# A selective scan and a convolution with attention, float32 on one core: the first layer's gates are stored before silu, and a new order is planned batch by batch

## The chip, the core and the metric

The kernel runs on one core of a Trainium2 chip. Engines are named as in the profile: PE (TensorE, matrix products and transposes), DVE (VectorE), ACT (ScalarE), POOL (GpSimd) and SP (SyncE, which here only issues DMAs). All data are float32. The metric is the device time of one execution in microseconds (us); lower is better.

## The reference

The input x is (4, 512, 32, 32): four batches, 512 channels, 1024 tokens. Two layers, each added to its input after a group normalisation `_gn`:

```
x = x + L0(_gn(x))      # selective scan
x = x + L1(_gn(x))      # convolutions and attention
# L0, per batch, 1024 tokens, 1024 inner channels, 16 states
xm, z = layernorm(x) @ W_in, split in two
xs    = silu(conv1d(xm, 4 taps) + conv_b)
dt    = softplus(xs @ W_x[:, :32] @ W_dt + b_dt);  Bm, Cm = the other 32 columns
h[t]  = exp(dt[t] * A) * h[t-1] + (dt[t] * xs[t]) * Bm[t]      # 16 states a channel
y     = sum over states of h * Cm + xs * D
out   = (y * silu(z)) @ W_out
```

L1 is a 3x3 convolution, an attention over the 1024 tokens by two 1x1 convolutions, and another 3x3 convolution; its 3x3 convolutions are done with transformed filters.

## The kernel before, in words

**Tiling of the first layer.** Channels lie on the 128 partitions, so the 1024 inner channels are 8 chunks d, taken in pairs e; the 1024 tokens are two halves h of 512. A *group* is (batch b, pair e, half h) and does 16 *units*, one for each state s; 4 x 4 x 2 x 16 = 512 units.

**A unit** (`unit`, L844 to L951) has one of two forms, by the table `ACT_B` in `shares` (L302). *On ACT*: ACT scales the transposed dt·x by the state's B, four instructions (L875); PE turns the result back into a `u` bank of PSUM, eight transposes (L901); ACT writes the decay exp(dt·A) (L862). *Off ACT*: POOL multiplies dt·x by a broadcast row of B that SP loads (`bbc`, L890), and ACT writes the decay into the `u` banks. Then DVE scans, two instructions (L915). The product with C is POOL's (L938, one instruction for both chunks) or, for as many of the off-ACT units as `DVE_C` says, DVE's (L931, two), which then also copies the carry (L920). PE adds each chunk's product, transposed, into the banks `y0` and `y1` (L948).

**The end of a group** (`gate`, L956 to L1003): SP loads the pair's gates for this half (`szl`, L965), ACT copies y0 and y1 into one tile `yt` (L971), PE turns each into an `mm` bank (L981), DVE adds xs·D (L988) and multiplies by the gates (L991), and SP stores the result (`gd`, L1000). In the last batch the product stays in `xs`.

**Gates** (`gates`, L727): for each chunk, PE projects both halves (`pz`), ACT copies them into `sz` (L735) and takes silu of the whole (L739), and SP stores it to DRAM (`szd`, L743). The gates of batch b + 1 are made during batch b.

**Other work in the layer**: `norms` (group and layer norm), `conv1` and `conv1_half` (projection, four taps, silu at L685 and L723), `params` (B, C and dt's inputs), `delta` (softplus at L813, dt·x, its transposes), `out_proj` and `last_proj` (W_out), `transform` (18 pieces of the second layer's filters, on POOL, L1208 to L1228, as filler) and `first_image`. Softplus, silu and exp need different tables on ACT; a load is recorded at the line that asks for it, and a return to exp at L210.

**What sets the order.** Nothing is issued where it is written: each `step` goes to a planner (`Plan`, L60 to L172) with its engine, an assumed duration, a priority (a lower number is more urgent; unit s of group n of batch b has 128 b + 16 n + s) and the buffers it takes. `issue` (L108) plays the engines forward with these durations, with `LAG` and `HOP` between engines, `LOAD` for a table and `kb / 300 + 2.0` for a DMA, and issues the steps in the order that results. `AHEAD` bounds how far a step may run before the most urgent open one. A step that needs another table is put back by 5.46 x 1.3 unless it is more urgent than the others by 2.66. On the chip each engine, SP too, then runs its own list in order and waits where data or buffers are late. `PRM` holds the offsets of the priorities, `slots` the buffers of each ring: `mm` 2 and `u` 4 (PSUM), `y0` and `y1` one each, `sz`, `szl`, `yt` 1, `h` and `dbx` 4, `cbc` 5, `bb` 3, `xt` 1.

**The start.** Before the plan, L214 to L345 issue loads: `gmat` and x on SP, `w_top`, `w_center` and their biases on POOL (L223 to L227), and on ACT the two bias rows `brow` (L233), each scaled by -12 on ACT (L236), then nine small ones (`small`, L313, and L331 and L338). ACT takes exp of `a_log` (L327) and DVE negates it (L328).

Of the kernel before, what the change touches and what calls it, by code (L numbers as in the profile page):

```python
# [30 lines left out]
PRM = dict(tf=-22.1, pg=0.35, kt=2.5, ke=2.06, ka=-1.93, fl=0, fi=-4.54, m0=42.67, n0=49.76, nl=1.48, q0=67.23, qg=4.59, c0=60.23, cg=6.17, p0=114.55, e0=1.02, eg=7.73, g0=80.83, gg=9.09, o0=14.49, og=6.33, dl=12.15, t0=8, tg=57.65)  # L31


ACT_B = ((12, 9, 10, 9, 9, 10, 9, 9), (11, 9, 12, 8, 9, 8, 8, 8), (9, 9, 12, 12, 11, 12, 12, 13))
DVE_C = ((4, 7, 5, 1, 2, 3, 5, 5), (4, 3, 3, 2, 1, 5, 2, 4), (4, 4, 4, 4, 3, 1, 4, 2))
# [24 lines left out]
class Plan:  # L60
# [4 lines left out]
    LAG = {"PE": 0.2, "DVE": 0.08, "ACT": 0.1, "POOL": 0.06, "SP": 0.0}  # L65
    HOP, LOAD, SLACK, AHEAD = 0.05, 1.3, 0.11, 15.09
# [41 lines left out]
    def issue(self):  # L108
        ready = {e: [s for s in self.steps if s.eng == e and not s.unmet] for e in self.ENGINES}
        clock = {e: 0.0 for e in self.ENGINES}  # L110
# [4 lines left out]
        while left:  # L115
# [4 lines left out]
            for e in self.ENGINES:  # L120
                urgent = min((s.prio for s in ready[e] if s.table in (None, table)), default=1e9)
                found = []
                for s in ready[e]:
# [9 lines left out]
                    wait = t + (5.46 * self.LOAD if late and s.prio > urgent - 2.66 else 0.0)  # L133
# [25 lines left out]
            for b in s.bufs:  # L159
                b.left -= 1  # L160
                if b.ring and not b.left:
                    free[b.ring].append(s.done + self.HOP)
                    if b.done:
                        b.done(b.tile)
            ready[s.eng].remove(s)
            for u in s.users:
                u.unmet -= 1
                other = u.eng != s.eng or s.kb
                u.ready = max(u.ready, s.done + self.HOP if other else clock[s.eng])
                if not u.unmet:  # L170
                    ready[u.eng].append(u)
# [4 lines left out]
def mamba_then_pab_kernel(  # L176
# [46 lines left out]
    nc.gpsimd.dma_start(wt_sb[:, :, 0, :], w_top.rearrange("(c p) n -> p c n", p=P))  # L223
    nc.gpsimd.dma_start(wt_sb[:, :, 1, :], w_center.rearrange("(c p) n -> p c n", p=P))
    pb_sb = cpool.tile([P, 1], F32, tag="pb", name="pb_sb")
    nc.gpsimd.dma_start(pb_sb[0:PAB], b_top)
    nc.gpsimd.dma_start(pb_sb[PAB:P], b_center)  # L227


    brow = []  # L230
    for name, src in (("b", b_bottom), ("o", b_out)):
        t = cpool.tile([1, C], F32, tag=f"brow_{name}", name=f"brow_{name}")
        nc.scalar.dma_start(  # L233
            t.rearrange("o (c p) -> o c p", p=P), src.rearrange("p (c o) -> o c p", o=1)
        )
        nc.scalar.activation(t, t, AF.Copy, scale=-12.0)  # L236
        brow.append(t)
# [46 lines left out]
    with ExitStack() as l0:  # L284
# [7 lines left out]
        first_x = xtp.tile([P, NCC, L], F32, tag="xt", name="xt_0", bufs=1)  # L292
        for c in range(NCC):
            nc.sync.dma_start(first_x[:, c, :], x[0, c * P : (c + 1) * P].rearrange("p h w -> p (h w)"))

# [6 lines left out]
        def shares(b, n):  # L302

            k = min(b, 1) + (b == B - 1)
            rest = NS - ACT_B[k][n]
            off = [int((i + 0.5) * (NS - 1) / rest) for i in range(rest)]
            c = DVE_C[k][n]
# [20 lines left out]
        nc.vector.tensor_scalar_mul(a_sb, a_sb, -1.0)  # L328
# [21 lines left out]
        def dram_set(name, shape, n=B):  # L350
# [8 lines left out]
            "xt": 1, "xs": 10, "win": 2, "yt": 1, "dt": 2, "dtx": 2, "dtxt": 2, "cbc": 5,  # L359
            "sc": 2, "h": 4, "sz": 1, "bb": 3, "dbx": 4, "szl": 1, "wpr": 2, "res": 2,  # L360
# [7 lines left out]
        MM, TR = 0.88, 0.114  # L368
        ROWS, EXP, SCAN = 0.8, 0.61, 1.18
# [27 lines left out]
        xts, ready, xs, xh, dts = {}, {}, {}, {}, {}  # L397
# [21 lines left out]
        def norms(b, prio, lag=0.0):  # L419

            t = xts[b] = buf("xt", [P, NCC, L], f"xt_{b}")
            if b == 0:
                t.make = lambda: first_x
            src = x[b].rearrange("(c p) h w -> p c (h w)", p=P)
            xin = [buf(None, None, "") for c in range(NCC)]
            step("SP", 0.0, lambda: t(), [], [], prio, holds=[t])
            for c in range(NCC):
                step(
                    "SP", 0.3,
                    lambda c=c: b and nc.sync.dma_start(t()[:, c, :], src[:, c, :]),  # L430
                    [], [xin[c]], prio, kb=512, holds=[t],
                )
# [6 lines left out]
            for c in range(NCC):  # L439
# [9 lines left out]
                step("DVE", 1.4, stats, [xin[c]], [stat], prio, holds=[t])  # L449
# [15 lines left out]
            step("DVE", 0.6, mid, [], [pm, stat], prio)  # L465
# [47 lines left out]
            step("PE", 0.6, shift_mean, [stat], [pv], prio)  # L513
# [61 lines left out]
            for h, (r, pvar) in enumerate(zip(rs, pvars)):  # L575
                at = prio if b else at_half[h]
                step(
                    "ACT", 0.58,
# [74 lines left out]
        def conv1(b, d, prio):  # L653
# [5 lines left out]
            for at, end in ((0, 341), (341, 682), (682, L)):  # L659
# [22 lines left out]
                step("DVE", 0.25 + n * 0.0042, taps, [p], xsh, prio, holds=[u])  # L682
            step(
                "ACT", 1.06,
                lambda: nc.scalar.activation(u(), u(), AF.Silu, bias=cb_sb[:, d : d + 1]),  # L685
                [], xsh, prio, "silu", holds=[u],
# [40 lines left out]
        def gates(b, d, prio):  # L727

            w = load_win(b, NDC + d, prio)
            sz = buf("sz", [P, L], f"sz_{b}_{d}")  # L730
            for h, hs in enumerate(halves):
                p = project(b, NDC + d, w, f"pz_{b}_{d}_{h}", hs, prio)
                step(
                    "ACT", 0.48,
                    lambda hs=hs, p=p: nc.scalar.copy(sz()[:, hs], p()),  # L735
                    [p], [sz], prio,
                )
            step(
                "ACT", 0.97, lambda: nc.scalar.activation(sz(), sz(), AF.Silu),  # L739
                [], [sz], prio, "silu",  # L740
            )
            step(
                "SP", 0.3, lambda: nc.sync.dma_start(szd[b][d // 2][:, d % 2, :], sz()),  # L743
                [sz], [szds[b][d]], prio, kb=512,
            )

        def params(b, prio, hh=tuple(range(NH))):
# [4 lines left out]
            for n, h in enumerate(hh):  # L752
                hs = halves[h]
                pp = buf("mm" if b or h else "y0", [P, T], f"pp_{b}_{h}")
                for d in range(NDC):
# [7 lines left out]
                        prio + PRM["pg"] * (d + NDC * n) if b else prio - 0.05 * (NDC - d),  # L763
# [979 lines left out]
```

## Time and profile before

| | us |
|---|---|
| Median of three runs | 2928.78 (2926.93 to 2932.84) |
| The profiled execution | 2926.95 |
| Its span, first to last instruction | 2925.1 |
| End of the first layer's last group (second `yt` copy) | 1886.9 |
| From there to the end | 1038.2 |
| PE busy in the span | 2724.9 |
| DVE busy | 2292.1 |
| POOL busy | 2045.6 |
| ACT busy | 1831.1 |
| Loads of ACT tables, 153 of 1.283 | 196.3 |

The span is cut in 40 equal slices of 73 us, and a digit is the busy share of a slice in tenths, 9 for 90% or more. A line of a group of instructions reads: line, engine, operation, output<-inputs with shapes and count | busy us, mean ns of one | idle us of the engine just before them, and who ended it.

### The profile page before, as it was taken

How to read it: one execution, taken by the hardware profiler on the slowest of the kernel's cores; microseconds unless marked ns; L12 is line 12 of the kernel's file. 1: busy time of each engine (PE TensorE's matmuls, PEld its weight loads, DVE VectorE, ACT ScalarE, POOL GpSimd, SP SyncE). 2: the span in 40 equal slices, each digit the busy share in tenths (PEclk: the TensorE clock that was granted, in tenths of full speed). 3: DMA queues.
4: the chain of work that ended last, by engine and by line, in shares of the span. 5: the costliest groups of instructions: out<-in, count | busy, mean ns of one | idle time of the engine just before them, and what ended most of it. 6: DMA issues, size and time to landing. Idle time of an engine off the chain costs nothing.

```text
span 2925.1 us, 36166 instructions
## 1 busy us (share of the span) xinstructions
PE 2724.9 (93%) x11712; PEld 1615.4 (55%) x11712; DVE 2292.1 (78%) x2719; ACT 1831.1 (63%) x3248; POOL 2045.6 (70%) x1247
## 2 busy tenths in 40 slices
PE   5988899999899999899999989799999999999998
PEld 2456566666666666666656666544444444444444
DVE  4679899988999989999979999867776655346254
ACT  4689899998799999889998999630200003030000
POOL 6899898899998999998999999733141341214222
PEclk9999899999999999999999999999999999999999
DMA  6856555467545577655567654757789886536487
GB/s 168 235 155 199 165 158 166 152 213 242 195 140 165 172 213 246 200 150 152 175 204 216 219 172 147 160 217 263 256 277 290 307 329 242 200 124 236 162 319 259
DMA packets 405348, 603.94 MB, mean 206 GB/s; under 512 B 46088, under 2 KB 245000, under 8 KB 380584
## 3 DMA queue, kind: packets, MB, share of 16 engines
q1 hardware_dynamic: 396352, 587.11, 62.5%
q10 hardware_dynamic: 8648, 14.26, 1.4%
q8 instruction: 94, 1.54, 0.2%
q14 instruction: 94, 0.77, 0.1%
q0 software_dynamic: 160, 0.26, 0.0%
HBM read 504.53 MB, written 96.99 MB: 206 GB/s over the span
## 4 chain that ended last, share of the span: by engine, by line
PE 34%; DVE 7%; POOL 6%; ACT 5%; issue 3%; DMA 2%; SPq 0%; DVEq 0%; POOLq 0%; ACTq 0%
PE m_o L1533 11%; PE m_b L1533 8%; PE pat L1585 6%; POOL da L938 2%; PE y L948 2%; PE po L412 2%; DVE da L915 2%; PE u L901 1%; ACT sc L875 1%; PE psc L1385 1%; ACT da L862 1%; POOL dbx L890 1%; DMA uw_o<-u_o 1%; POOL dbx L938 1%; DMA u_o<-wr 1%
## 5 line engine op out<-in xcount | busy, mean ns | idle before, releaser
L938 POOL TENSOR_TENSOR da<-da,cbc 128x1024 f32<-128x1024 f32 x313 | 739.9, 2369 | 46.1 <-DVE da L915 32.8
L875 ACT ACTIVATE sc<-dtxt,bt_sb 128x256 f32<-128x256 f32 x1252 | 550.5, 498 | 22.6 <-PE u L901 21.6
L890 POOL TENSOR_TENSOR dbx<-dtx,bbc 128x1024 f32<-128x1024 f32 x199 | 469.9, 2371 | 26.5 <-PE y L948 12.9
L862 ACT ACTIVATE da<-dt,a_sb 128x512 f32<-128x512 f32 x626 | 431.2, 713 | 25.4 <-PE y L948 24.4
L915 DVE TENSOR_TENSOR_SCAN da<-da,u 128x512 f32<-128x512 f32 x328 | 383.8, 1203 | 26.2 <-PE u L901 16.9
L901 PE MATMUL u<-ident,sc 128*128 128x128 f32 x2504 | 363.0, 277 | 34.1 <-DVE da L915 13.8
L948 PE MATMUL y<-ident,da 128*128 128x128 f32 x2504 | 348.8, 279 | 48.9 <-POOL da L938 45.8
L901 PEld LDWEIGHTS u<-ident,sc 128*128 128x128 f32 x2504 | 293.5, 142 | 168.3 <-issue 64.3
L915 DVE TENSOR_TENSOR_SCAN da<-da,carry_sb,u 128x512 f32<-128x512 f32 x298 | 365.2, 1259 | 19.8 <-PE u L901 15.6
L948 PEld LDWEIGHTS y<-ident,da 128*128 128x128 f32 x2504 | 287.7, 143 | 132.3 <-POOL da L938 101.6
L1533 PE MATMUL m_o<-uw_o,v_o 128*128 128x512 f32 x768 | 336.4, 597 | 8.3 <-DMA uw_o<-u_o 8.2
L1533 PE MATMUL m_b<-uw_b,v_b 128*128 128x512 f32 x768 | 333.7, 593 | 4.8 <-ACT e_b L1541 2.2
L862 ACT ACTIVATE u<-dt,a_sb 128x512 f32<-128x512 f32 x398 | 264.9, 681 | 13.9 <-DVE da L915 8.9
L412 PE MATMUL pxm<-xt,winc 128*128 128x345 f32 (+3 forms) x704 | 240.9, 485 | 11.2 <-DMA winc<-in_w_in_dram 4.0
L1533 PEld LDWEIGHTS m_o<-uw_o,v_o 128*128 128x128 f32 x768 | 145.3, 191 | 190.9 <-issue 179.8
L1533 PEld LDWEIGHTS m_b<-uw_b,v_b 128*128 128x128 f32 x768 | 144.9, 190 | 189.9 <-issue 178.9
L412 PE MATMUL pz<-xt,winc 128*128 128x512 f32 x512 | 244.0, 596 | 6.0 <-DMA winc<-in_w_in_dram 2.0
L948 PE MATMUL y<-ident,dbx 128*128 128x128 f32 x1592 | 221.0, 276 | 8.7 <-POOL dbx L938 7.3
L938 POOL TENSOR_TENSOR dbx<-dbx,cbc 128x1024 f32<-128x1024 f32 x93 | 220.6, 2372 | 10.7 <-DMA bbc<-bcd 5.4
L1585 PE MATMUL pat<-y_b,st 128*128 128x512 f32 x512 | 223.3, 597 | 1.6 <-DVE rz L1594 1.6
L948 PEld LDWEIGHTS y<-ident,dbx 128*128 128x128 f32 x1592 | 183.3, 142 | 49.5 <-POOL dbx L938 19.6
L1541 ACT ACTIVATE e_o<-m_o 128x512 f32<-128x512 f32 x24 | 14.3, 597 | 276.8 <-PE m_o L1533 276.8
(229 smaller groups left out, 4259.2 us busy)
## 6 DMA issues: line engine op xcount, KB each, us to landing
cbc<-bcd SPq DMA_DIRECT2D x512, 256.0 KB, 3.7
uw_b<-u_b SPq DMA_DIRECT2D x96, 1024.0 KB, 4.8
uw_o<-u_o SPq DMA_DIRECT2D x96, 1024.0 KB, 4.8
bbc<-bcd SPq DMA_DIRECT2D x199, 256.0 KB, 4.0
u_b<-work SPq DMA_DIRECT2D x192, 128.0 KB, 2.8
winc<-in_w_in_dram SPq DMA_DIRECT2D x72, 256.0 KB, 3.9
szd<-sz SPq DMA_DIRECT2D x32, 512.0 KB, 3.6
szl<-szd SPq DMA_DIRECT2D x32, 512.0 KB, 5.1
```

Source lines behind the costliest of these rows:

```text
L412: lambda k=k, lhs=lhs, rhs=rhs: nc.tensor.matmul(p()[:, at : at + cols], lhs(), rhs(), start=(k == 0), stop=(k == n - 1)),
L862: nc.scalar.activation(t, dt()[:, j], AF.Exp, scale=a_sb[:, at : at + 1])
L875: nc.scalar.activation(sc()[:, k], dtxt()[:, k], AF.Copy, scale=bt[:, at, s : s + 1])
L890: lambda: nc.gpsimd.tensor_mul(hc(), dtx(), b_bc().to_broadcast([P, 2, T])),
L901: nc.tensor.transpose(u()[:, k * P : (k + 1) * P], sc()[:, k, j, :], ident)
L915: nc.vector.tensor_tensor_scan(ht, *((hc()[:, j], u()) if on_act else (u(), hc()[:, j])), carry_sb[:, j, s : s + 1] if h else 0.0, ALU.mul ...
L938: nc.gpsimd.tensor_mul(hc(), hc(), c_bc().to_broadcast([P, 2, T]))
L948: nc.tensor.matmul(y[j]()[:, k, :], hc()[:, j, k * P : (k + 1) * P], ident, start=(s == 0 and k == 0), stop=(s == NS - 1 and k == NK - 1), ...
L1385: nc.tensor.matmul(pt, top[:, m * P : (m + 1) * P], center[:, h * T : (h + 1) * T], start=True, stop=True,)
L1533: nc.tensor.matmul(m[q], v[:, q, k, c, :], w[:, c, :], start=(c == 0), stop=(c == NCC - 1 and not extra),)
L1541: nc.scalar.activation(e, m[2], AF.Copy, scale=al / 2)
L1585: nc.tensor.matmul(pt, st[m][:, 2 * P * j + h : 2 * P * (j + 1) : 2], xb[m // 2][:, m % 2, :], start=(m == 0), stop=(m == NMC - 1),)
```

## The change

It does six things in the first layer.

1. **Gates.** `gates` copies each half from PSUM into a tile `z` of 512 columns and stores it raw. A new step, `gate_inputs`, loads a pair of chunks, both halves, into `sz` (2 x 1024 columns) and takes silu there in one instruction; both halves' groups use it. The buffers: `z` one, `sz` one, `szl` none.
2. **`yt`** is one tile for each chunk in place of one for both, and its ring still has one buffer, now of half the size.
3. **The convolution's silu** is a step of its own, for one or two chunks at a time (`xp`: two for batches 1 and 3, one for batch 2).
4. **Shares.** `ACT_B` and `DVE_C` have a row for each batch. On ACT: 77, 73, 73, 90 units before, 70, 74, 73, 90 after. C products on DVE: 32, 24, 24, 26 before, 33, 30, 32, 28 after.
5. **Order.** Offsets for each batch, a priority for each filter piece, new durations, lags and hops, engines that start at other times, and 1.06 in place of 5.46 for another table.
6. **Small loads.** The second layer's weights and biases are loaded by SP within the plan at priority 300, and the bias rows are scaled by ACT after the plan; x's first load is a step of the plan at priority -100; `a_sb` is negated on ACT.

The diff's core (the steps whose durations alone change are left out):

```diff
-PRM = dict(tf=-22.1, pg=0.35, kt=2.5, ke=2.06, ka=-1.93, fl=0, fi=-4.54, m0=42.67, n0=49.76, nl=1.48, q0=67.23, qg=4.59, c0=60.23, cg=6.17, p0=114.55, e0=1.02, eg=7.73, g0=80.83, gg=9.09, o0=14.49, og=6.33, dl=12.15, t0=8, tg=57.65)
-ACT_B = ((12, 9, 10, 9, 9, 10, 9, 9), (11, 9, 12, 8, 9, 8, 8, 8), (9, 9, 12, 12, 11, 12, 12, 13))
-DVE_C = ((4, 7, 5, 1, 2, 3, 5, 5), (4, 3, 3, 2, 1, 5, 2, 4), (4, 4, 4, 4, 3, 1, 4, 2))
+PRM = dict(
+    zl=(17.12, 2.32, 10.64, 9.46),
+    zs=(-6.6, 6.76, 2.95, 4.73),
+    xp=(2, 1, 2),
+    d1=4.6,
+    pg=(0.27, 0.49, 0.44, 0.21),
+    kt=(4.63, 8.03, 4.61, 4.92),
+    ke=(1.37, 5.31, 5.42, 3.82),
+    ka=(-2.99, -1.21, -2.32, -1.96),
+    dl=(11.98, 8.7, 12.71, 6.84),
...
+    g0=(-2.52, -46.63, -47.32, -52.32),
+    gg=(7.13, 9.33, 9, 9.19),
...
+    pc=(-90.27, -21.17, 5.21, -51.1, -41.83, -34.43, -45.01, 14.16, -32.58, 66.75, 105.34, 148.87, 209.89, 261.18, 327.32, 394.8, 432.73, 495.28),
...
+)
+ACT_B = (
+    (11, 9, 11, 9, 8, 7, 7, 8),
+    (11, 8, 13, 8, 8, 7, 10, 9),
+    (11, 8, 10, 10, 11, 7, 8, 8),
+    (9, 12, 10, 12, 11, 11, 11, 14),
+)
+DVE_C = (
+    (5, 4, 3, 4, 3, 2, 8, 4),
+    (4, 6, 3, 2, 2, 6, 2, 5),
+    (5, 4, 5, 2, 2, 6, 3, 5),
+    (7, 2, 3, 4, 3, 2, 5, 2),
+)
-    LAG = {"PE": 0.2, "DVE": 0.08, "ACT": 0.1, "POOL": 0.06, "SP": 0.0}
-    HOP, LOAD, SLACK, AHEAD = 0.05, 1.3, 0.11, 15.09
+    LAG = {"PE": 0.17, "DVE": 0.095, "ACT": 0.1, "POOL": 0.06, "SP": 0.0}
+    HOP = {"PE": 0.16, "DVE": 0.045, "ACT": 0.06, "POOL": 0.08, "SP": 0.05}
+    BEGIN = {"PE": 5.0, "DVE": 1.5, "ACT": 9.0, "POOL": 7.0, "SP": 1.5}
+    FREE, LOAD, SLACK, AHEAD = 0.06, 1.3, 0.11, 15.64
+    TURN, URGENT = 1.06, 2.68
-                    wait = t + (5.46 * self.LOAD if late and s.prio > urgent - 2.66 else 0.0)
+                    wait = t + (self.TURN * self.LOAD if late and s.prio > urgent - self.URGENT else 0.0)
+    def load_l1():
+        for k, w in enumerate((w_top, w_center)):
+            nc.sync.dma_start(wt_sb[:, :, k, :], w.rearrange("(c p) n -> p c n", p=P))
...
+        for t, src in zip(brow, (b_bottom, b_out)):
+            nc.sync.dma_start(
+                t.rearrange("o (c p) -> o c p", p=P), src.rearrange("p (c o) -> o c p", o=1)
+            )
-        nc.vector.tensor_scalar_mul(a_sb, a_sb, -1.0)
+        nc.scalar.activation(a_sb, a_sb, AF.Copy, scale=-1.0)
-            "xt": 1, "xs": 10, "win": 2, "yt": 1, "dt": 2, "dtx": 2, "dtxt": 2, "cbc": 5,
-            "sc": 2, "h": 4, "sz": 1, "bb": 3, "dbx": 4, "szl": 1, "wpr": 2, "res": 2,
+            "xt": 1, "xs": 10, "win": 2, "dt": 2, "dtx": 2, "dtxt": 2, "cbc": 5,
+            "sc": 2, "h": 4, "sz": 1, "z": 1, "yt": 1, "bb": 3, "dbx": 4, "wpr": 2, "res": 2,
         def gates(b, d, prio):
             w = load_win(b, NDC + d, prio)
-            sz = buf("sz", [P, L], f"sz_{b}_{d}")
             for h, hs in enumerate(halves):
                 p = project(b, NDC + d, w, f"pz_{b}_{d}_{h}", hs, prio)
...
+                z = buf("z", [P, T], f"z_{b}_{d}_{h}")
+                step("ACT", 0.468, lambda z=z, p=p: nc.scalar.copy(z(), p()), [p], [z], prio)
+                step(
+                    "SP", 0.3,
+                    lambda z=z, hs=hs: nc.sync.dma_start(szd[b][d // 2][:, d % 2, hs], z()),
+                    [z], [szds[b][d]], prio, kb=256,
+                )
+        def gate_inputs(b, e):
+            prio = (b * NDC + 2 * e) * NS + PRM["zl"][b]
+            sz = szs[b, e] = buf("sz", [P, 2, L], f"sz_{b}_{e}")
+            step(
+                "SP", 0.3, lambda: nc.sync.dma_start(sz(), szd[b][e]),
+                szds[b][2 * e : 2 * e + 2], [sz], prio, kb=1024,
+            )
+            step(
+                "ACT", 1.99, lambda: nc.scalar.activation(sz(), sz(), AF.Silu),
+                [], [sz], prio + PRM["zs"][b], "silu",
+            )
         def gate(b, e, h, y):
-            yt = buf("yt", [P, 2, NK, P], f"yt_{name}")
+            sz = szs[b, e]
+            yt = [buf("yt", [P, NK, P], f"yt_{name}_{j}") for j in range(2)]
             for j in range(2):
                 step(
-                    "ACT", 0.48, lambda j=j: nc.scalar.copy(yt()[:, j], y[j]()),
-                    [y[j]], [yt], prio - 0.5,
+                    "ACT", 0.468, lambda j=j: nc.scalar.copy(yt[j](), y[j]()),
+                    [y[j]], [yt[j]], prio - 0.5,
                 )
...
         norms(0, -20)
+        step("SP", 1.6, load_l1, [], [], 300, kb=64)
...
+                if not h:
+                    gate_inputs(b, e)
                 for s in range(NS):
                     unit(b, e, h, s, y)
...
             plan.issue()
+        for t in brow:
+            nc.scalar.activation(t, t, AF.Copy, scale=-12.0)
```

## The prediction, made before the changed kernel was run

> **What bounds the kernel now.** I read the busy tenths first: the first layer fills the first 26 slices, the second the other 14, where PE alone is full.
>
> ```profile
> span 2925.1 us, 36166 instructions
> ...
> PE   5988899999899999899999989799999999999998
> ...
> DVE  4679899988999989999979999867776655346254
> ACT  4689899998799999889998999630200003030000
> POOL 6899898899998999998999999733141341214222
> ```
>
> In the first layer PE, DVE, ACT and POOL are all at eight or nine tenths: no single bound, but four that take turns. So I cut it where a group of 16 units ends, at the second of its two `yt` copies in ACT's timeline: after the first group (198.7) and after batches 0, 1, 2 and 3 (600.6, 1052.0, 1506.9, 1886.9). Busy times by stage, columns us and (x instructions):
>
> ```profile
> core 0: us, PE busy (x) PEld busy (x) DVE busy (x) ACT busy (x) POOL busy (x), PEclk, DMA share, GB/s
> 198.70:600.60 401.90, 366.68 (x2011) 252.55 (x2010) 376.65 (x448) 389.19 (x669) 357.72 (x209) 0.97 0.55 168
> 600.60:1052.00 451.40, 423.44 (x2298) 288.13 (x2296) 411.56 (x474) 414.24 (x727) 423.70 (x255) 0.98 0.61 189
> 1052.00:1506.90 454.90, 426.72 (x2310) 292.17 (x2310) 408.17 (x468) 418.78 (x731) 429.11 (x262) 0.99 0.61 188
> 1506.90:1886.90 380.00, 343.49 (x2131) 252.49 (x2130) 364.88 (x394) 346.76 (x667) 371.74 (x229) 0.98 0.63 189
> ```
>
> Batch 0 is **ACT's** (12.7 idle of 401.9); batches 1 and 2 are PE's and POOL's together (26 to 28 idle), ACT and DVE 36 to 47; batch 3 is POOL's (8.3 idle), DVE next (15.1).
>
> Third, the groups of instructions, which give the prices (busy us, mean ns, idle before):
>
> ```profile
> L938 POOL TENSOR_TENSOR da<-da,cbc 128x1024 f32<-128x1024 f32 x313 | 739.9, 2369 | 46.1 <-DVE da L915 32.8 <-POOL carry_sb L937 0.2
> L875 ACT ACTIVATE sc<-dtxt,bt_sb 128x256 f32<-128x256 f32 x1252 | 550.5, 498 | 22.6 <-PE u L901 21.6
> L931 DVE TENSOR_TENSOR dbx<-u,cbc 128x512 f32<-128x512 f32 x212 | 138.6, 670 | 0.0
> L210 ACT ACT_TABLE_LOAD x67 | 86.0, 1283 | 1.8 <-PEq L1733 0.7
> L739 ACT ACT_TABLE_LOAD x29 | 37.2, 1283 | 0.5
> ```
>
> Mean times overlap with their neighbours, so I price by busy over count: a unit's B-scaling on ACT is four L875, 4 x 0.440 = 1.76; a POOL product 2.37; a unit's C-product on DVE two L931, 1.31; one of the 8 transposes that an ACT unit needs 363.0/2504 = 0.145 (L901); a table load 1.283. Last, the waits of the first 30 us:
>
> ```profile
> ACT brow_b L236 <- DMA brow_b<-in_b_bottom_dram: 12.0, 1, 12.0
> ...
> DVE a_sb L328 <- ACT a_sb L327: 4.6, 1, 4.6
> ```
>
> **What the Trainium skill says.** "ScalarE: Activation LUTs", What ACT_TABLE_LOAD costs: 1283 ns per load plus about 1380 ns of drain. The load agrees; the drain does not show (load at 24.99, next activation at 26.29), so I price 1.283. The same section gives an activation with immediate operands 186 + 0.833 N ns: 1039 at N = 1024, where the gates' silu shows 1059 (33.9/32). "GPSIMD Engine Reference", 4.1 Engine selection: two-input elementwise work is about twice as slow on GpSimd; here 2.37 for 1024 columns against 1.31, so a product moved to DVE takes less than it gives. "DMA: Bandwidth & Descriptors", Rules for kernel authors: a load whose last dimension isn't contiguous becomes one descriptor per element; the two 2 KB rows of `brow` show it, still awaited at 13.96 after an issue at 0.76, with the next load on ACT's queue held 8.45 in its issue.
>
> **The change, part by part**, against the profiled run (2926.95, span 2925.1; the median shown is 2928.78, so 1.8 is added at the end).
>
> *Start (to 198.7).* Now ACT waits for `brow` until 13.96, and the loads issued behind it on its queue, `a_log` among them, land late. Its exponential runs at 19.35, DVE's negation waits 4.6 for it, and the last statistics (data done at 15.07) stand behind that, at 19.84. With `brow` gone and the negation on ACT they follow at about 15.1: 4.7 gained. Then ACT stands 4.4 for the first filter piece, whose load SP held 8.4 for `lnw`; that load goes with the rest: ACT was ready for the logarithm at 22.06 and ran its table load at 24.99. 4.7 + 2.9 = 7.6 at most. x itself shares the transfers with the now earlier small loads: 0 at least. I take **-6**.
>
> *Batch 0 (198.7 to 600.6).* ACT: the shares of groups 1 to 7 fall from 65 to 59 units, 6 x 1.76 = 10.6. Silu: 12 singles here (6 of them for batch 1's gates) become three of batch 0's pairs; a pair costs 1.059 + 1024 x 0.833 ns = 1.91, so 12.7 - 5.7 = 7.0. Table loads: now 18 L210, 12 L739, 8 L685, 7 L813 = 45; after, 3 gate pairs, 4 convolution pairs, 7 softplus = 14, each with at most one return, 28: 17 x 1.283 = 21.8. ACT 389 - 39 = 350. POOL takes the 6 units: +6 x 2.36 = 14, 372. DVE keeps 28 C-products, 377. PE 6 x 8 x 0.145 = -7, 360. DVE becomes the bound, and ACT's saving beyond 12 is worth nothing. With 12.7 idle, as the bound has now, 389 (-12); with DVE's present 25, no gain: **-7**. If the table loads stay, ACT is at 372 and still not the bound.
>
> *Batch 1.* Shares 73 to 74, C-products on DVE 24 to 30. POOL -7 x 2.37 = -16.6 (407), DVE +7.9 (420), ACT about -4 (four loads fewer; the unit's 1.8; silu -0.8) (410), PE +1.2 (425). PE stays: only its waits for POOL can shrink: **-2**.
>
> *Batch 2.* C-products 24 to 32, and one filter piece (12.0: three L1208-like of 1.82 and nine of 0.73) goes to batch 3: POOL -31 (398), DVE +10.5 (419), ACT -10 loads and -0.8 = -14 (405), PE 427. **-5**.
>
> *Batch 3.* POOL +12.0 for the piece (priority 394.8, past 384), -2 x 2.37: +7.3 (379); DVE +2.6 and copies of carries +1 (368.5); ACT four pairs 7.6 for two silus 2.1 and about five loads 6.4: +12 (359, cover: 33 idle). POOL is the bound: +7, less what batch 2's freed POOL does ahead: **+4**.
>
> *Waits added.* The gate store is split: 32 issues more on SP, 16 gate loads fewer, 6 B-rows more (0.32 each, in SP's waiting time). `z` has one buffer: the second half's copy waits for the first half's store, and behind it on ACT stand exponentials and scalings, while `pz` holds one of two `mm` banks: 0 to 32 x 1 us; I take 0, since the priorities put other work between. The six small loads on SP in mid-layer can hold `cbc` loads up to 12 once; five `cbc` buffers cover five units of 3.5 us: 0, and 12 if that cover is used up. The two `brow` scalings (1.26) go into ACT's idle 3.1 ahead of L1433. `yt` has one half-buffer: see the slower rival; 0 in the sum. SP's x loads stay first.
>
> *Order.* The lags, hops and durations by which the planner orders everything change, and offsets become each batch's own. The trace of before cannot show it. The bounds' idle time is 12.7 + 28 + 26 + 8 = 75; batch 3 shows 2% is possible. Bounds -40 (batches 1 and 2 at batch 3's share) and +20 (a worse order by a quarter); I take **-16**.
>
> Sum: -6 - 7 - 2 - 5 + 4 - 16 = -32: 2926.95 - 32 + 1.8 = **2897**. The second layer (1038.2 to the end) is untouched.
>
> **The rivals.**
> *PE takes over.* For: PE is within 1 us of POOL in batch 1 and loses nothing there. Then batches 0 to 2 give nothing, batch 3 costs 7, the start gives 6: 2926.95 + 1 + 1.8, about 2930. Against: 45.8 of PE's waits are for POOL's L938.
> *The order pays fully.* Batches 1 and 2 idle like batch 3: -6 - 12 - 18 - 18 - 2 = -56, 2873. For: the filler pieces and gates have slack. Against: those batches carry projections through two `mm` banks, which batch 3 does not.
> *Slower: the serial drain of y.* ACT's second `yt` copy now waits until PE has turned the first. At 490.96 both copies run back to back (1.05), and the first four turns end at 493.92; with 0.58 for the copy y1 would come free at 494.5 instead of 492.0, 2.5 late. PE runs in order; its adds into y1, and POOL and DVE behind their tiles, wait. 31 boundaries x 2.5 = 78 at most, 2975; the gain of 32 is gone from 1.0 each on. I take half of it, 2897 + 39 = 2936. Against: PE can turn at once and other work fills in.
>
> **How the numbers follow.** Forecast 0.58 (own range 2880 to 2920), full order 0.20, PE takes over 0.10, drain 0.12. About 0.2% (6 us) is what can be told from no change. Faster 0.58 + 0.20 = 0.78, same 0.10, slower 0.12. The range 2866 to 2930 leaves out the drain and the far end of the full order.
>
> **What would show it.** Table loads about 100 to 130 in place of 153; ACT no longer the busiest of batch 0; the last statistics near 15; batch 3 longer by some us; the second `yt` copy no more than 1 us later than now. Wrong if PE's waits for ACT's `yt` exceed 30 us, if ACT waits for `z`'s store, or if the binding engine's idle time in batches 1 and 2 stays above 28.

## The result and the profile after

Over 20 executions of each, the changed kernel takes 2921.68 us (2913.54 to 2929.93) and the kernel before 2926.71: a ratio of 0.9984, interval 0.9975 to 0.9993. It is about 5 us faster; the forecast was 32. The profiled execution of after took 2919.48 (span 2917.7) against 2926.95, so its trace accounts for 7.4.

The page of after, busy tenths in 40 slices:

```profile
span 2917.7 us, 36108 instructions
...
PE   6888899999999999999999998799999999999998
...
DVE  4679999998999889999999899967777665346264
ACT  4779998898898898998999999630200003030000
POOL 6889999998988899988999999733141341214222
```

The picture is that of before: 26 slices in which four engines are nearly full. The first layer cut at the same places, the second `yt` copy of a group (L1012 now):

```profile
core 0: us, PE busy (x) PEld busy (x) DVE busy (x) ACT busy (x) POOL busy (x), PEclk, DMA share, GB/s
...
202.80:596.30 393.50, 357.28 (x1948) 248.59 (x1947) 378.58 (x455) 350.44 (x617) 369.19 (x212) 0.97 0.56 172
596.30:1052.40 456.10, 429.40 (x2324) 295.69 (x2323) 420.63 (x492) 412.30 (x725) 412.17 (x252) 0.97 0.59 187
1052.40:1492.90 440.50, 419.74 (x2304) 289.87 (x2303) 421.18 (x501) 402.77 (x712) 402.69 (x237) 0.99 0.63 194
1492.90:1881.90 389.00, 348.40 (x2116) 254.27 (x2114) 362.05 (x395) 360.59 (x672) 371.05 (x231) 0.98 0.62 183
1881.90:2917.70 1035.80, 1005.93 (x2428) 450.52 (x2428) 615.52 (x766) 136.47 (x241) 304.61 (x142) 0.99 0.71 248
```

Two columns are to be read against each other. The busy times came out nearly as worked out: batch 0 was to be PE 360, DVE 377, ACT 350, POOL 372, and is 357, 379, 350, 369; batches 1 to 3 are within 8 of the forecast on every engine. The lengths did not follow. What the busiest engine leaves idle is 393.5 - 378.6 = 14.9 (DVE), 26.7 (PE), 19.3 (DVE) and 17.9 (POOL): 79 in all, where before it was 12.7 + 28 + 26 + 8 = 75. The forecast took 16 out of that.

| stage | before | after | difference | forecast, without Order |
|---|---|---|---|---|
| to the first group's end | 198.7 | 202.8 | +4.1 | -6 |
| batch 0 | 401.9 | 393.5 | -8.4 | -7 |
| batch 1 | 451.4 | 456.1 | +4.7 | -2 |
| batch 2 | 454.9 | 440.5 | -14.4 | -5 |
| batch 3 | 380.0 | 389.0 | +9.0 | +4 |
| second layer | 1038.2 | 1035.8 | -2.4 | 0 |

So -7.4 = -32 + 16 (Order, which did not come) + 10 (the start) - 2 (second layer) + 1 (the batches: -9.1 for -10). Each length is read from one trace. Three more traces of kernels that do the same work in the same order in the first group (`loads_back`, `brow_late` and `brow_late_two`, below) end it at 198.9, 198.6 and 200.1 in place of 202.8, so a stage of a single trace is good to some 4 us, and the smaller differences of the table are not clear of chance.

The groups that the parts were priced by:

```profile
L983 POOL TENSOR_TENSOR da<-da,cbc 128x1024 f32<-128x1024 f32 x307 | 725.5, 2367 | 43.7 <-DVE da L960 24.2
L920 ACT ACTIVATE sc<-dtxt,bt_sb 128x256 f32<-128x256 f32 x1228 | 538.9, 498 | 50.5 <-PE u L946 49.5
L976 DVE TENSOR_TENSOR dbx<-u,cbc 128x512 f32<-128x512 f32 x246 | 161.2, 672 | 0.0
L252 ACT ACT_TABLE_LOAD x60 | 77.0, 1283 | 1.7 <-PEq L1783 0.7
L788 ACT ACTIVATE sz<-sz 128x2048 f32<-128x2048 f32 x16 | 30.6, 1911 | 0.2
```

Returns to exp fell from 67 to 60, all table loads from 153 to 125 (by batch 25, 34, 30 and 21, before 45, 40, 40 and 15); a pair's silu takes the 1.91 that was estimated. And ACT's scalings now wait 49.5 for PE's transposes (L946), where before they waited 21.6: ACT's idle time grew where its work shrank.

### The profile page after: what moved, and what is told of

Same layout as the page of the kernel before. It is cut to its first block, busy times and chain, and to the rows that moved or that the text cites. A ratio compares the mean times of both kernels' runs of the same rounds, so it can differ in the third digit from the quotient of the medians.

```text
span 2917.7 us, 36108 instructions
## 1 busy us (share of the span) xinstructions
PE 2726.0 (93%) x11664; PEld 1622.0 (56%) x11664; DVE 2319.7 (80%) x2776; ACT 1791.6 (61%) x3181; POOL 2018.2 (69%) x1220
## 4 chain that ended last, share of the span: by engine, by line
PE 48%; DVE 26%; ACT 9%; POOL 6%; issue 6%; DMA 5%; SPq 0%; DVEq 0%; ACTq 0%; POOLq 0%
PE m_o L1583 11%; PE m_b L1583 8%; DVE da L960 8%; PE pat L1635 6%; PE y L993 5%; DVE u L960 4%; PE u L946 4%; PE pz L447 3%; DVE dbx L960 3%; DVE xs L709 3%; PE po L447 3%; POOL da L983 2%; ACT sc L920 2%; ACT da L907 2%; DVE dbx L976 2%
## 5 line engine op out<-in xcount | busy, mean ns | idle before, releaser
L983 POOL TENSOR_TENSOR da<-da,cbc 128x1024 f32<-128x1024 f32 x307 | 725.5, 2367 | 43.7 <-DVE da L960 24.2
L920 ACT ACTIVATE sc<-dtxt,bt_sb 128x256 f32<-128x256 f32 x1228 | 538.9, 498 | 50.5 <-PE u L946 49.5
L935 POOL TENSOR_TENSOR dbx<-dtx,bbc 128x1024 f32<-128x1024 f32 x205 | 483.7, 2369 | 19.1 <-PE y L993 9.8
L907 ACT ACTIVATE da<-dt,a_sb 128x512 f32<-128x512 f32 x614 | 420.9, 713 | 23.0 <-PE y L993 21.6
L946 PE MATMUL u<-ident,sc 128*128 128x128 f32 x2456 | 368.1, 282 | 44.1 <-DVE da L960 25.2
L960 DVE TENSOR_TENSOR_SCAN da<-da,u 128x512 f32<-128x512 f32 x320 | 375.1, 1204 | 27.4 <-PE u L946 16.2
L946 PEld LDWEIGHTS u<-ident,sc 128*128 128x128 f32 x2456 | 291.2, 144 | 188.3 <-issue 64.6
L960 DVE TENSOR_TENSOR_SCAN da<-da,carry_sb,u 128x512 f32<-128x512 f32 x294 | 360.8, 1261 | 17.1 <-PE u L946 13.1
L993 PE MATMUL y<-ident,da 128*128 128x128 f32 x2456 | 341.1, 278 | 24.5 <-POOL da L983 22.2
L907 ACT ACTIVATE u<-dt,a_sb 128x512 f32<-128x512 f32 x410 | 272.2, 681 | 24.0 <-DVE da L960 13.1
L447 PE MATMUL pz<-xt,winc 128*128 128x512 f32 x512 | 247.1, 607 | 14.7 <-DVE xs L749 4.3
L993 PE MATMUL y<-ident,dbx 128*128 128x128 f32 x1640 | 235.4, 279 | 11.8 <-DVE dbx L976 5.2
L993 PEld LDWEIGHTS y<-ident,dbx 128*128 128x128 f32 x1640 | 194.3, 144 | 47.5 <-issue 22.7
L983 POOL TENSOR_TENSOR dbx<-dbx,cbc 128x1024 f32<-128x1024 f32 x82 | 194.0, 2366 | 5.4 <-POOL da L983 2.3
```

The source lines that it names most:

```text
L447: lambda k=k, lhs=lhs, rhs=rhs: nc.tensor.matmul(p()[:, at : at + cols], lhs(), rhs(), start=(k == 0), stop=(k == n - 1)),
L907: nc.scalar.activation(t, dt()[:, j], AF.Exp, scale=a_sb[:, at : at + 1])
L920: nc.scalar.activation(sc()[:, k], dtxt()[:, k], AF.Copy, scale=bt[:, at, s : s + 1])
L935: lambda: nc.gpsimd.tensor_mul(hc(), dtx(), b_bc().to_broadcast([P, 2, T])),
L946: nc.tensor.transpose(u()[:, k * P : (k + 1) * P], sc()[:, k, j, :], ident)
L960: nc.vector.tensor_tensor_scan(ht, *((hc()[:, j], u()) if on_act else (u(), hc()[:, j])), carry_sb[:, j, s : s + 1] if h else 0.0, ALU.mul ...
```

## The experiments

Two theories stood at first, and each expectation below numbers its own versions of them. One: the time follows the planner, and an order holds only in the durations that it was planned and tuned with; the new ones are too short for the chip, so what the parts give is lost again. The rival: the engines' work sets the time, what a plan gains is washed out by the waits, and the missing gain lies in a part: the start given back on the way, the serial drain of `yt`, or saved table loads that were off the path. Each ratio is to the kernel before, run beside it.

### The start alone

The kernel before with its own plan, and from the change only the small loads on SP at priority 300 and `a_sb` negated on ACT.

```diff
-        nc.vector.tensor_scalar_mul(a_sb, a_sb, -1.0)
+        nc.scalar.activation(a_sb, a_sb, AF.Copy, scale=-1.0)
...
+        step("SP", 1.6, load_l1, [], [], 300, kb=64)
```

> The kernel before with the small loads alone changed: the second layer's weights and biases loaded by SP within the plan, the bias rows scaled after it, a_sb negated on ACT; the plan's other steps keep their order. Theory 1 (the prediction's first step holds, and what was lost between 60 and 203 us was lost by the new order): the normalisation's logarithm runs 5 to 6 us earlier and the whole kernel is 6 us faster, 2921 beside 2927. Theory 2 (the first group has slack, so an earlier start is swallowed whatever the order): the logarithm is as much earlier, the first group ends at 198 as before, and the time is 2927 within 2.

2919.91 against 2923.34: 0.9985 (0.9977 to 0.9994), some 4 us, 2 to 7 within the interval. In its trace the first group ends at 190.8 in place of 198.7 and the last at 1881.0 in place of 1886.9: in the order of before, most of what the start gains passes through the whole layer, as the first theory has it. In after the head starts as early; its timeline on DVE:

```profile
12.31 1.29 DVE L479 BATCH_NORM_STATS2 bs_l<-xt 128x6 f32<-128x512 f32 x2 [2.68 <-DMA xt<-in_x_dram]
13.63 0.21 DVE L480 BATCH_NORM_AGGREGATE mv_l<-bs_l 128x2 f32<-128x12 f32 x1
```

The last statistics stand at 13.63 (19.84 before, about 15.1 in the forecast), and the logarithm at 20.00 in place of 26.29. The first group loses it again: its waits between 60 and 203 us in after are

```profile
DVE da L960 <- PE u L946: 19.1, 6, 9.8
...
POOL carry_sb L982 <- DVE da L960: 9.1, 2, 8.3
```

(us in total, times, longest): DVE's scans, and POOL behind them, stand for transposes that PE does late. In the same stretch of before these two waits were 5.5 and 2.2.

### The structure alone, and the order alone

`structure_only` is the kernel before with the change of gates, `yt` and silu, planned with the old numbers (the two new steps have the new offsets `zl` and `zs`). `order_only` is the changed kernel with the old `gates` and `gate` put back (each chunk's silu before its store) and one chunk a silu step, planned with the new numbers:

```diff
-    xp=(2, 1, 2),
+    xp=(1, 1, 1),
...
-                z = buf("z", [P, T], f"z_{b}_{d}_{h}")
-                step("ACT", 0.468, lambda z=z, p=p: nc.scalar.copy(z(), p()), [p], [z], prio)
...
+                "ACT", 0.97, lambda: nc.scalar.activation(sz(), sz(), AF.Silu),
+                [], [sz], prio, "silu",
```

> The kernel before with the buffers and steps alone changed (raw gates, silu on a loaded pair, one half-size yt buffer, one z buffer, the convolution's silu in pairs for batches 1 and 3), with the old shares, offsets and durations, and the new offsets zl and zs for the two new steps. The planner's own clock puts the end of the first layer's last group 42 us later than before (1870.7 for 1829.1). Theory 1 (the work sums decide): about 30 table loads go, ACT is relieved in batch 0 where it binds, some 10 us faster, 2917. Theory 2 (the planner's clock passes through to the chip): 2968. Theory 3 (the single yt and z buffers cost by themselves): 2940 to 2960, with PE or ACT waiting for yt and z.

> The changed kernel with the old gates, yt and single silu steps put back, so that the new start, shares, offsets, lags and durations are what is left of the change. Theory 1 (the new order loses on the chip what its shares gain): 2925 to 2937, no faster than before, with the losses between 60 and 203 us and in batches 1 and 3. Theory 2 (the order pays, and the structure took it back): 2905 or less. The planner's clock puts its last group at 1829.1, 33 later than the changed kernel's, so if that clock passes through it is at 2955.

Measured: 2975.92, 1.0168 (1.0148 to 1.0188), and 2956.11, 1.0109 (1.0091 to 1.0126). Either half by itself costs 32 to 49; together they give 5. The theory that the planner's clock passes through (2968 and 2955) comes nearest in both. The single buffers are not enough to account for it: in the trace of `structure_only` PE and its weight loads for `y` stand 22 in all for `yt`, and ACT 8.0 for `z`'s store, where in after, with the same buffers, it is 13.9 and 7.0. Neither half was searched anew, so the two are priced with offsets that were tuned for something else, not at their best. Offsets, durations and structure belong together, and the change has no sum of parts as far as the order goes.

### The old offsets in the first group

After, with the offsets of batch 0's first group (`d1`, `d2`, `h0`, `hg`, `p1`, `g0[0]`, `gg[0]`, the first nine of `pc`) as before.

```diff
-    d1=4.6,
+    d1=9.6,
...
-    p1=0.19,
-    d2=-10.04,
+    p1=8.6,
+    d2=20.02,
```

> The changed kernel with the offsets of batch 0's first work as before (the second half's convolutions, the first deltas, batch 0's gates, the first nine filter pieces). Theory 1 (the new offsets of the first group lose the 10 us that the start gains and more): the first group ends at about 193 instead of 203, and the time is 2912. Theory 2 (the loss is chance of the order, or is given back in batch 0, which DVE binds): first group anywhere from 193 to 203, time 2920 to 2925; the planner's clock says 3 later than the changed kernel.

2919.16 against 2923.34: 0.9982 (0.9973 to 0.9990). The first group ends at 193.9 in place of 202.8 and batch 0 at 586.6 in place of 596.3; of these 10, 5.5 are left at 1876.4 in its trace, and the ratio can't be told from that of after. The first theory's 193 came, its 2912 did not. The new offsets lose part of the start's gain in the first group (5 to 9 us, since other traces of after's order end it at 198.6 to 200.1), but keeping it is worth little in this order.

### The durations alone

The kernel before with nothing changed but the planner's durations, lags, hops and starting times, and `AHEAD` (15.64 in place of 15.09), and planned again with them:

```diff
-        MM, TR = 0.88, 0.114
-        ROWS, EXP, SCAN = 0.8, 0.61, 1.18
+        MM, TR = 0.858, 0.109
+        ROWS, EXP, SCAN = 0.8, 0.613, 1.12
...
-                step("DVE", 0.25 + n * 0.0042, taps, [p], xsh, prio, holds=[u])
+                step("DVE", 0.25 + n * 0.0037, taps, [p], xsh, prio, holds=[u])
```

> The kernel before with the planner's durations, lags, hops and starting times of the change, and nothing else: same buffers, shares, offsets, loads. The planner re-orders with them. Its last group ends at 1833.5 by the new durations (before's own order, played in the new durations, ends at 1835.8), and at 1883.1 when the same order is played in the old durations (before's: 1829.1). Theory 1 (the new durations are nearer to the chip, so their clock passes through): 2921 to 2925. Theory 2 (each order fits the durations that it was planned with, and the chip lies between the two): the mean of -2 and +54, +26, so 2949, with more idle time on PE, DVE and ACT alike in every batch.

2961.19 against 2924.15: 1.0126 (1.0107 to 1.0146), 37 slower. The same instructions run; from the first group's end to the last, the kernel before and this one:

```profile
198.70:1886.90 1688.20, 1560.32 (x8746) 1085.35 (x8746) 1561.27 (x1784) 1568.97 (x2790) 1582.28 (x952) 0.98 0.60 184
```

```profile
203.90:1916.80 1712.90, 1570.53 (x8745) 1100.39 (x8744) 1560.88 (x1783) 1566.20 (x2781) 1582.31 (x952) 0.97 0.58 181
```

DVE, ACT and POOL are busy within 3 us of before, and the stage is 24.7 longer: for them it is idle time. PE, with the same instructions, is busy 10.2 longer, at a granted clock of 0.97 in place of 0.98. The two programs differ in their order alone, and the loss is more than the 26 of the second theory. Another 5.2 is in the first group; the last 7, in the second layer (1045.5 in place of 1038.2), is not explained.

### The old durations on the changed kernel

The mirror image: after with the old durations, offsets and shares kept, planned again.

```diff
-        MM, TR = 0.858, 0.109
-        ROWS, EXP, SCAN = 0.8, 0.613, 1.12
+        MM, TR = 0.88, 0.114
+        ROWS, EXP, SCAN = 0.8, 0.61, 1.18
```

> The changed kernel planned with the durations, lags and hops of the kernel before, offsets and shares kept. Theory 1a (a set of offsets is good only with the durations that it was tuned with): the fitted clock ends at 1912.4 against 1871.6, so about 2950 to 2962. Theory 2a (the old durations are simply nearer the chip's, whatever the offsets): not slower than the changed kernel, 2900 to 2922.

2959.33 against 2926.36: 1.0109 (1.0092 to 1.0126). So "the old durations are nearer the chip and would do better" falls, though for the longest groups they are nearer (below). What fits both this run and the one before it is that offsets are good only with the durations that they were tuned in.

### A reshuffle that means nothing

> The kernel before with AHEAD 15.0 in place of 15.09, planned anew: a reshuffle that means nothing. The planner's own clock ends it 8.7 later, the fitted clock 9.8 later (1886.4 against 1876.6). Theory 1 (the planner's clock passes through): 7 to 12 over the kernel before. Theory 2 (any order but the tuned one costs 30 or more): 30 to 50 over it. Theory 3 (small differences of the plan are washed out): within 3.

```diff
-    HOP, LOAD, SLACK, AHEAD = 0.05, 1.3, 0.11, 15.09
+    HOP, LOAD, SLACK, AHEAD = 0.05, 1.3, 0.11, 15.0
```

2930.65 against 2926.36: 1.0015 (1.0007 to 1.0022), 4 slower, 2 to 6 within the interval: less than the first theory, far less than the second, and not clear of the third's 3. In the planner's clock the order is the same until about 1205, for SP's loads until about 1005, so only the last third or so of the layer was reshuffled. Batches 2 and 3 of its trace:

```profile
1045.80:1503.50 457.70, 426.74 (x2304) 292.90 (x2304) 408.95 (x468) 423.18 (x733) 429.28 (x262) 0.99 0.61 186
1503.50:1888.30 384.80, 345.62 (x2135) 253.02 (x2134) 369.73 (x403) 348.34 (x669) 371.95 (x229) 0.99 0.64 189
```

They are 2.8 and 4.8 longer than before, 7.6 of the plan's 9, while the first group and batches 0 and 1, whose order is the same, are some 2 shorter each, by chance. So the trace is closer to the planner's clock than the ratio is, and not every order but the tuned one costs 30; what a reshuffle of the whole layer would cost isn't shown.

### The table loads put back

After in its own order, with a load of exp's table behind each silu of the convolution and of a pair of gates, where it wasn't there anyway: 156 loads in place of 125, 40 us of ACT.

```diff
+                exp_set()
...
-                "ACT", 1.99, lambda: nc.scalar.activation(sz(), sz(), AF.Silu),
+                "ACT", 1.99, lambda: (nc.scalar.activation(sz(), sz(), AF.Silu), exp_set()),
```

> The changed kernel, its order kept, with an exp table loaded straight after each silu of a pair: 31 table loads more, 31 x 1.283 = 40 us of ACT. Theory 1 (the prediction: ACT has stopped being a bound, and the loads that the change saves are worth little): within 8 us of the changed kernel. Theory 2 (ACT's order is tight, so its work passes on to the others): 20 to 40 us slower, 2940 to 2960, most of it in batches 0 and 1.

2948.43 against 2924.15: 1.0083 (1.0064 to 1.0102), 27 to 29 over after: the second theory. Its stages, same columns:

```profile
198.90:595.20 396.30, 358.03 (x1949) 249.35 (x1948) 379.01 (x455) 358.05 (x624) 369.09 (x212) 0.97 0.55 171
595.20:1066.40 471.20, 430.96 (x2324) 296.84 (x2323) 421.84 (x492) 429.49 (x737) 412.06 (x252) 0.97 0.58 182
1066.40:1515.40 449.00, 423.71 (x2304) 290.87 (x2303) 421.50 (x501) 413.49 (x720) 402.43 (x237) 0.98 0.61 191
```

In batch 0, six loads (7.7) cost 2.8: DVE is ahead of ACT there. In batch 1, thirteen loads (16.7) cost 15.1, and ACT's 429.5 of 471.2 is still not full: 42 idle. In batch 2 eight (10.3) cost 8.5, in batch 3 four (5.1) cost 4.8. The first group, where no load was added, is 3.9 shorter than in after's trace, so none of the four prices is finer than some 4 us; together they are 31 for 40. An engine with 40 us of idle time in a stage passed on about nine tenths of what it was given.

### One buffer or two for `yt` and `z`

To make room, both kernels load the bias rows where the second layer begins; the second then has two buffers for `yt` and for `z`, in the same order.

```diff
-                lambda: pool.tile(shape, F32, tag=ring, name=name, bufs=plan.slots[ring]),
+                lambda: pool.tile(shape, F32, tag=ring, name=name, bufs=2 if ring in ("yt", "z") else plan.slots[ring]),
```

> The changed kernel with the two bias rows loaded and scaled at the second layer's start, which frees 4 KB of SBUF a partition in the first; its order is kept. It is the base for the next kernel. Both theories: within 4 us of the changed kernel, later if anything, at the second layer's start.

> The same with two buffers for yt and two for z, in the same order of issue, so that only waits go. Theory 1 (the serial drain of y and the single z buffer are covered): 0 to 4 us faster than the same kernel with one buffer of each. Theory 2 (the slower rival: the second yt copy, now 0.5 to 20 us behind the first, holds up PE): 10 us faster or more, with the waits of PE for yt (15 us together) and of ACT for z's store (7 us) gone.

2919.69 (0.9993, 0.9980 to 1.0007) and 2917.16 (0.9982, 0.9972 to 0.9992): 2.5 apart. The intervals overlap, so the pair shows only that the second buffers are worth little, as the first theory has it. The waits of after between 202.8 and 1881.9 say why:

```profile
PEld y L993 <- ACT yt L1012: 8.7, 14, 1.2
ACT z L772 <- DMA szd<-z: 7.0, 6, 1.9
PE y L993 <- ACT yt L1012: 5.2, 10, 1.0
```

The copies do run apart (3.7 us from start to start in the middle case, 868.7 and 889.4 in the worst group, where before it was mostly 0.5), but PE waits 0.5 to 0.6 a time.

### Durations fitted to the chip

After with its planner's durations scaled (one factor for each kind), lags and hops until the clock, played through the orders of six of the kernels above, ended their groups where the traces do; then offsets, shares and filler priorities searched anew in that clock.

```diff
+FIT = {"TR": 0.837, "MM": 1.116, "DV": 1.14, "EXP": 1.014, "ROWS": 0.983, "AC": 1.041}
...
-        s = Step(eng, us, fn, prio, table, kb, fill)
+        s = Step(eng, fitted(eng, us), fn, prio, table, kb, fill)
...
-    (11, 9, 11, 9, 8, 7, 7, 8),
+    (12, 10, 11, 10, 9, 8, 7, 8),
```

> The changed kernel with the planner's durations, lags and hops scaled so that, played through six orders measured above, they give those kernels' own group ends (matrix products x1.12, DVE's work other than scans x1.14, ACT's copies x1.04, transposes x0.84), and with offsets, shares and filler priorities searched anew in that clock. In the fitted clock the changed kernel's order ends its last group at 1871.6, this one at 1843.5. Theory 1 (what Order was to give is lost because the new durations are shorter than the chip's): most of the 28 shows, 2894 to 2908, faster than both kernels. Theory 2 (engines' waits wash out what a plan gains, and any order other than the two tuned ones costs 30 or more, as the others did): 2920 or more.

> The same order as refit, with two buffers in place of one for yt and z, and the bias rows loaded where the second layer begins. Theory 1: as in the pair measured before, 2 to 5 less than refit, 2890 to 2905. Theory 2: within 2 of refit or above it.

`refit` takes 2903.22 against 2926.36: 0.9921 (0.9909 to 0.9934). `refit_two` takes 2900.68: 0.9912 (0.9899 to 0.9926). Both beat both kernels, and both are inside the first theory's range; after stood at 0.9984. The trace of `refit` is of the fastest of its six executions (2897.85), 5 below their median. Its stages:

```profile
198.20:581.50 383.30, 351.88 (x1975) 245.01 (x1973) 371.69 (x444) 352.60 (x627) 361.67 (x210) 0.99 0.56 173
581.50:1033.60 452.10, 422.25 (x2327) 294.49 (x2327) 417.72 (x485) 411.49 (x726) 427.55 (x262) 0.98 0.62 192
1033.60:1474.20 440.60, 419.19 (x2288) 289.93 (x2287) 416.51 (x488) 401.28 (x702) 403.92 (x235) 0.98 0.62 192
1474.20:1858.20 384.00, 347.31 (x2161) 257.44 (x2159) 357.52 (x384) 366.28 (x694) 368.11 (x232) 0.99 0.61 181
```

From the first group's end to the last it takes 1660.0, after 1679.1. Of these 19, some 14 are work that the busiest engine of each batch no longer has (371.7 for 378.6, 427.6 for 429.4, 419.2 for 421.2, 368.1 for 371.1), and 5 its idle time (11.6, 24.6, 21.4 and 15.9: 73.5 for 79). The work went off DVE: with longer durations for all that it does but the scans, the search gives it 110 products with C, where after has 123 and before 106, and ACT 316 units (after 307). The first group ends 4.6 earlier. The structure is after's, and so nearly are the table loads (123).

All nine orders together. The clocks are the planner's own `issue`, played through each kernel's order with the old, the new and the fitted durations; "chip" is the second `yt` copy of the last group in the trace (all as the start of that copy):

| kernel | old | new | fitted | chip |
|---|---|---|---|---|
| before | 1829.1 | 1835.8 | 1876.6 | 1886.9 |
| after | 1857.6 | 1795.8 | 1871.6 | 1881.9 |
| structure_only | 1870.7 | 1872.8 | 1923.6 | 1933.5 |
| order_only | 1888.1 | 1829.1 | 1910.1 | 1915.0 |
| old_head | 1861.2 | 1799.2 | 1874.4 | 1876.4 |
| before_durations | 1883.1 | 1833.5 | 1905.7 | 1916.8 |
| after_durations | 1874.3 | 1859.6 | 1912.4 | 1922.7 |
| null_before | 1837.8 | 1844.4 | 1886.4 | 1888.2 |
| refit | | | 1843.5 | 1858.2 |

Read the first two rows: in its own clock after is 40 better than before (1835.8 to 1795.8), in the old clock 28 worse; the chip says 5 better, as the fitted clock does. The last three rows had no part in the fit, and it places them 10.3, 1.8 and 14.7 under the chip (the six others 2 to 11).

The entry of `refit`, 1843.5, is the one in its expectation. The planner in the file of `refit`, with the constants that stand there, ends this order at 1821.1 (and after's order at 1873.1), 37 before the chip. So an order looks best in the clock in which it was searched, and even the fitted clock promised its own order 52, of which 24 came. The fit isn't a list of measured durations either: it shortens a transpose to 0.84 x 0.109 = 0.091, where after's trace has 368.1/2456 = 0.150 (L946).

## Why the prediction was wrong

**The failed step is "Order: I take -16".** The parts' work came out as priced, and the idle time that the order was to reduce went from 75 to 79. The prediction took a gain for the new lags, hops and durations without asking whether they are nearer the chip; it said that the trace of before cannot show it. For the longest groups they aren't nearer: in the trace of after, for the units on ACT, a scan that starts from a carry takes 360.8/294 = 1.23 and one without 375.1/320 = 1.17, planned at 1.12 (1.18 before); three convolution taps take 3 x 0.567 = 1.70, planned at 1.51 (1.68 before); two matrix products of 512 columns 2 x 247.1/512 = 0.97, planned at 0.858 (0.88 before).

```profile
L960 DVE TENSOR_TENSOR_SCAN da<-da,u 128x512 f32<-128x512 f32 x320 | 375.1, 1204 | 27.4 <-PE u L946 16.2 <-ACT da L907 10.4
L960 DVE TENSOR_TENSOR_SCAN da<-da,carry_sb,u 128x512 f32<-128x512 f32 x294 | 360.8, 1261 | 17.1 <-PE u L946 13.1 <-ACT da L907 4.0
L709 DVE SCALAR_TENSOR_TENSOR xs<-pxm,cw_sb,xs 128x342 f32<-128x342 f32 x72 | 40.9, 567 | 3.2 <-ACT xs L700 1.3
L447 PE MATMUL pz<-xt,winc 128*128 128x512 f32 x512 | 247.1, 607 | 14.7 <-DVE xs L749 4.3 <-DVE xs L709 3.1 <-DMA winc<-in_w_in_dram 2.8
```

What the runs show in place of the -16: these durations in before's own plan cost 37 with the same instructions, the old ones in after's plan cost about as much against after (1.0109 for 0.9984), and a search in a clock fitted to the traces gains some 18 over after (0.9921). How the harm comes about is argued and not shown: a plan with too short a time for DVE and PE counts on their results before they are there, and hands DVE work that the others had room for; on the chip the engines run their lists in order and wait. The slip from the own clock to the chip grew from 1886.9 - 1829.1 = 58 to 1881.9 - 1795.8 = 86; part of it is the search, since `refit` slips by 37 in its own clock. The rows stand in the profile of before too (its scans are 365.2/298 and 383.8/328, the same 1.23 and 1.17) and showed that the new durations are further off; the step took a value between two bounds instead. Its lower bound, too, is mis-summed: batches 1 and 2 at batch 3's 2.2% of idle time give 27.7 - 9.8 and 25.8 - 9.9, so -34 and not -40.

**Start, -6:** the mechanism and the size were right (`start_only`: -6 at the layer's end, -4 over all executions). In after it is lost by 202.8; `old_head` shows that the new offsets of the first group do most of that, and up to 4 us is the chance of one trace.

**Batch 0, -7:** right (-8.4), ACT 350 to the microsecond and DVE the bound. "ACT's saving beyond 12 is worth nothing" holds roughly there: loads put back cost 0.36 of their time.

**Batches 1 and 2, -2 and -5:** the terms took ACT's fewer loads for nothing, since PE and POOL were the bounds. `loads_back` prices them at nine and eight tenths of their time. With its prices the loads alone give, by stage, 20 fewer x 1.283 x 0.36 = 9, 6 x 1.283 x 0.90 = 7, 10 x 1.283 x 0.83 = 11, and six more in batch 3 cost 6 x 1.283 x 0.94 = 7: a gain of 20, and 26 with the start. The measured 5 then leaves some 21 that the order, the shares and the buffers take together. (In that experiment the order stayed, so a new plan might have absorbed part, the prices are those of after and not of before, and each carries the 4 us of a single trace: 20 is a rough estimate.)

**Batch 3, +4:** the sign was right, and it is +9: POOL's work stayed (371.74 to 371.05, the forecast was 379), and POOL's idle time rose from 8 to 18. The filter piece came as told, but POOL does some six products fewer in this stage, not two: three of batch 3's products with B were done before batch 2 ended.

**Waits added, 0:** 2.5 for `yt` and `z` together, not clear of zero. ACT did wait for `z`'s store, 7.0 in six waits, so "0, since the priorities put other work between" was a little low.

**The rivals.** *PE takes over* has the total nearly right (2930), but not the place: batch 1 is PE's (26.7 idle), while batch 2, where it saw no gain, fell by 14. *The serial drain of y* exists, at 0.5 to 0.6 a wait and not 2.5. *The order pays fully* did not come: the new durations alone cost 37. That the order could lose by its own durations was not among the rivals, and the signs that were set missed it: loads, ACT's share, the last statistics and batch 3 came as told; the second `yt` copy, which was to start no more than 1 us later, is later than that in every group and costs little; and of the three that were to mean "wrong" only the wait for `z`'s store appeared. The busiest engines' idle time, 75 to 79, was the sign that counted.

**Open.** `refit` changed durations, offsets and shares at once. Whether a fresh search in the new durations would have found as much, and what the old structure would give with fitted durations and its own search, was not tried; so of the 23 that `refit` gains over before, the structure's share is not settled. Nor is it settled which wrong duration does the harm, or whether it is the new values or only their mismatch with the offsets. The granted clock is a further rival for a part: in the same round its median was 0.987 for `refit` and 0.983 for before, and among the 27 executions of before one with 0.001 more is some 1.2 us shorter, so 4 to 5 of the 23 may go with it; no run shows what sets it. It can't be the main cause of the losses, since `after_durations` is 33 slower at before's 0.983.

## What to carry to other kernels

Where a planner orders the work, compare each assumed duration with the trace's (busy over count) before believing its clock, don't take the gain shown by the clock in which the order was searched as the gain on the chip, and expect tuned offsets to hold only with the durations that they were tuned in. An engine with a tenth of a stage idle isn't free when four engines feed one another in order: price what it saves by putting it back. A kernel's parts can be tuned to each other so that each alone costs 30 to 50 and both together gain 5; test a half before calling it a gain.

## What the runs showed of the hardware

A scan over 512 columns takes 1.17 from zero and 1.23 from a carry in SBUF (busy over count, above). And a tiny instruction of DVE on two SBUF inputs, 0.2 us otherwise, was held for as long as POOL's product ran; the timeline of after, start and duration first:

```profile
149.77 2.35 POOL L983 TENSOR_TENSOR da<-da,cbc 128x1024 f32<-128x1024 f32 x1
...
150.16 1.98 DVE L754 SCALAR_TENSOR_TENSOR xs<-tails,cw_sb,xs 128x3 f32<-128x3 f32 x1
```

Both end at 152.1. The Trainium skill, "SBUF — State Buffer", SBUF: two separate sides, says that a DVE operation with two SBUF inputs and a GpSimd one exclude each other for the whole instruction. The trace agrees here: POOL's started first, and DVE's ended with it. The 24 instructions of L754 take 0.205 to 1.99 us, 20.5 in all; the 24 of before take 13.3.
